# Depthwise convolution stage of a ConvNeXt block with a gate: matmul order kept as written, last 16 channels by halves of the images, norms ahead of their transposes

## The chip, the cores and the metric

The kernel runs on one core of one Trainium2 chip. The metric is device time in microseconds (us); the number for a kernel is the median of its runs. The kernel before takes 3158.46 us (three runs, 3158.37 to 3160.17). All data are float32.

## What is computed

The input x has 32 images of 384 channels and 28 x 28 pixels. Cut to what matters, the reference is:

```python
y = depthwise_conv7x7(x, dw_w) + dw_b            # padding 3, one 7x7 filter per channel
y = (y - mean_c(y)) * rsqrt(var_c(y) + 1e-6) * ln_g + ln_b   # over the 384 channels of a pixel
h = gelu(y @ w1 + b1)                            # 384 -> 1536
gx = sqrt(sum_pixels(h * h)); nx = gx / (mean_f(gx) + 1e-6)
h = grn_g * (h * nx) + grn_b + h
v = x + (h @ w2 + b2)                            # 1536 -> 384, residual
logits = concat(mean_hw(v) @ W1.T, group_max(v, W2_1) * W2_2, min_hw(v) @ W3.T) @ Wfc.T
out = sigmoid(logits[:, :, None, None] + v)
```

## The kernel before

**Engines.** PE (TensorE) does matmuls and transposes, ACT (ScalarE) and DVE (VectorE) empty PSUM and do element work, POOL (GpSimd) does element work in SBUF, SP only issues DMAs. A framework tracks which instruction needs which tile, inserts the semaphore waits, and also schedules: within an engine, instructions need not come in the order in which the Python code issues them, unless they are marked with `keep_in_program_order`. In the kernel before, none is marked.

**Stage 1: the convolution (L178 to L462).** The 7x7 filter of one channel becomes a banded matrix (`tmat`, loaded by `load_t`, L216, eight channels at a time, from a table of shifted taps `fs` in DRAM that is written at the start, L201 to L209). Pixels of four image rows, padded to 32 columns, lie on the 128 partitions; the seven such row blocks of 32 images are 224 columns. One channel is three matmuls into one PSUM area: the row block itself (L401, 224 columns), the block after (L402, 192 columns, 96 weight columns) and the block before (L405, 192). Each matmul shows as two records on PE.

The data come in with 32 channels of 4 images on the partitions: `load_x` (L235, on SP's queue, eight buffers `xi`), `pad_x` (L249: copied into one of two `xpad` buffers, by POOL for the first chunk at L253, then by ACT at L255), `turn_x` (L257: seven transposes at L264 into `pt`, three PSUM banks, in two halves, copied into `xt` by DVE at L272 or, in the first chunk, every second by ACT at L274). So stage 1 has 12 chunks of 32 channels, each chunk four steps `s` of eight channels, each step four pairs `c2` of two channels. While chunk k is convolved, the eight groups of chunk k + 1 are padded, turned and copied, one half-group after each pair. The result of a pair in `pc` (four banks) gets its bias on its way into `yc`, on DVE for odd pairs (L411) and on ACT for even ones (L419). Sixteen channels make a `yc`, which goes to DRAM: `yd` for the first 22 (L437), `yl` for the last 2 (L443), since the next stage wants all channels of one image. Image 0's part of the last channels is copied on the chip (L442) and its statistics taken (L441). Also in this stage, POOL forms sums of blocks of the two weight matrices (`form_w`, L324) and SP stores them to `u1d` and `u2d`.

**Between the stages (L867 to L873).** Image 0 is normalised: `stats` (L497), `std` (L509), then for each of seven row blocks j `norm` (L525, one instruction at L523 on ACT or L521 on DVE) and three transposes into `py` (L547, in `turn`); after j = 3 and j = 6 three copies take `py` to `acc` with scale and shift (L553). `forms_up` (L565, L587) makes ten sums and differences of `acc`'s blocks, on DVE for image 0 and on POOL for all others; they are the operands of the first matrix product, which is done in 15 block products instead of 18.

**Per image: `up` and `down`.** `up(b)` (L604) takes four tiles of the hidden layer in two pairs; for each pair it goes through the 15 entries of `UPSTEPS` (L92), two matmuls of 392 columns each (one a tile; two records a matmul, L627). An entry names the operand, the bank A, B or C that it adds to, and what is read from a bank afterwards (ACT copies at L634, DVE adds and subtracts at L636 to L644). `down(b)` (L696) is the second product, 15 entries of `STEPS`, four matmuls each (L717). All other work of the images is hung on these steps by two tables: `within(b)` (L794) for `up`, `beside(b)` (L832) for `down`: gelu (L596), squares (L602), scaling, the gate, and for image b + 2 the norms, transposes, evictions and `forms_up`. In the latter table, transposes of row blocks 0, 1 stand at step 0, of 2, 3 at step 1, of 4, 5 at step 2, of 6 at step 3; norms 0 and 1 are done in `up`, the others just ahead of their transposes. `yn`, the output of a norm, has three buffers.

Of the kernel before, what the change touches and what calls it, by code (L numbers as in the profile page):

```python
# [13 lines left out]
P = 128  # L14
# [50 lines left out]
)  # L65
EARLY = 7
# [26 lines left out]
    ("x", "+20", "A", 1, (("A", "copy", "2a"),)),  # L93
    ("p", "+20-21", "B", 1, (("B", "copy", "2b"),)),
    ("s", "-02", "C", 1, (("C", "copy", "0a"),)),
    ("v", "-12-20", "A", 0, (("A", "sub", "2b"),)),
    ("r", "-02+20-21", "B", 0, (("B", "sub", "2a"),)),
    ("2a", "-02+20+22", "C", 0, (("C", "add", "2a"),)),
    ("w", "-11+20", "A", 0, (("A", "copy", "E"),)),
    ("1a", "-01-20+21", "B", 0, (("B", "rsub", "E"),)),  # L100
    ("z", "-12", "C", 1, (("C", "add", "2b"),)),
# [20 lines left out]
def convnext_gate_kernel(  # L122
# [53 lines left out]


    with ExitStack() as one:  # L178
        tp = one.enter_context(tc.tile_pool(name="tp", bufs=1))
        xip = one.enter_context(tc.tile_pool(name="xip", bufs=8))  # L180
# [6 lines left out]
        ws = tp.tile([P, CB * FF], F32, name="ws")  # L187
        dww = tp.tile([P, CB, 49], F32, name="dww")
        nc.sync.dma_start(dww, dw_w.rearrange("(cb p) t -> p cb t", p=P))
        tab = tp.tile([P, CB, FL], F32, name="tab")  # L190
        dwb = tp.tile([P, C], F32, name="dwb")
        awt = tp.tile([P, 2, CB, R], F32, name="awt")
        w22b = tp.tile([P, R], F32, name="w22b")
        wfc = tp.tile([3 * R, C], F32, name="wfc")
        grp = tp.tile([P, CB, R], F32, name="grp")
        grp_a = tp.tile([P, CB, R], F32, name="grp_a")
# [5 lines left out]
        for cb in range(CB):  # L202
            nc.scalar.dma_start(fs[cb][P:, :], tab[:1, cb, :])
            nc.vector.tensor_copy(
                tab[:, cb, S0 : S0 + SN - 7].rearrange("p (y x) -> p y x", x=PW)[:, :, :7],
                dww[:, cb, :42].rearrange("p (y x) -> p y x", x=7),
            )
            nc.vector.tensor_copy(tab[:, cb, S0 + SN - 7 :], dww[:, cb, 42:])
            nc.scalar.dma_start(fs[cb][:P, :], tab[:, cb, :])  # L209
# [16 lines left out]
        NPAD = 2  # L226
# [4 lines left out]
        NG = B // NB  # L231
        GT = NX * NG
        xis = {}

        def load_x(i):  # L235

            k, g = divmod(i, NG)
            t = xis[i] = xip.tile([P, NT], F32, tag="xi", name=f"xi_{i}")
            base = x[g * NB, k * XC : k * XC + 1, :]
            nc.sync.dma_start(  # L240
                t,
                bass.AP(
                    tensor=base.tensor,
                    offset=base.offset,
                    ap=[[NT, XC], [C * NT, NB], [1, NT]],
                ),
            )
# [8 lines left out]

        def turn_x(i, h, xt, eng=nc.vector):  # L257
# [5 lines left out]
            for j in range(j0, j1):  # L263
                nc.tensor.transpose(  # L264
                    pt[:, j - j0, :],
                    xpad[i % NPAD][:, j * RW : (j + 1) * RW, :].rearrange("p r w -> p (r w)"),
                    ident,
                )
# [66 lines left out]

        AHEAD = NG
        for i in range(AHEAD):
            load_x(i)
        xt = new_xt(0)
        for i in range(NG):  # L340
# [4 lines left out]
            if i == NG - 2:  # L345

# [4 lines left out]
            for h in range(2):  # L351
                turn_x(i, h, xt, (nc.vector, nc.scalar)[h])

# [17 lines left out]
        GS = NG // SK  # L371
        for s in range(NK):
# [22 lines left out]
            t = tmat[s % NT2]  # L395
            for c2 in range(TC // 2):
                pc = psc.tile([P, 2, 256], F32, tag="pc", name=f"pc_{s}_{c2}")
                for ci in range(2):
                    c = 2 * c2 + ci
                    xc = xt[:, si * TC + c, :]  # L400
                    nc.tensor.matmul(pc[:, ci, :N], t[:, c, P : 2 * P], xc, start=True, stop=False)  # L401
                    nc.tensor.matmul(  # L402
                        pc[:REACH, ci, : N - B], t[:, c, 2 * P : T0 + MW], xc[:, B:], start=False, stop=False
                    )
                    nc.tensor.matmul(  # L405
                        pc[:, ci, B:N], t[:, c, :P], xc[:, : N - B], start=False, stop=True
                    )
                cc = s * TC + 2 * c2
                cy = cc % YC
                if c2 % 2:  # L410
                    nc.vector.tensor_tensor(  # L411
                        yc[:, :, :, cy : cy + 2].rearrange("p b j c -> p c j b"),
                        pc[:, :, :N].rearrange("p c (j b) -> p c j b", j=NJ),
                        dwb[:, cc : cc + 2].unsqueeze(2).unsqueeze(3).to_broadcast([P, 2, NJ, B]),
                        ALU.add,
                    )
                else:
                    for ci in range(2):
                        nc.scalar.activation(  # L419
                            yc[:, :, :, cy + ci].rearrange("p b j -> p j b"),  # L420
                            pc[:, ci, :N].rearrange("p (j b) -> p j b", j=NJ),
                            AF.Identity,
                            bias=dwb[:, cc + ci : cc + ci + 1],
                            scale=1.0,
                        )
                if xn is not None:
                    g, h = divmod(si * (TC // 2) + c2, 2)
                    i = (k + 1) * NG + g
                    if h == 0:
                        pad_x(i)  # L430
                        if i + AHEAD < GT:
                            load_x(i + AHEAD)
                    turn_x(i, h, xn)
            if s % 2:
                yv = yc.rearrange("p b j c -> p b (j c)")
                if kt < NY - NLAST:
                    nc.sync.dma_start(yd[:, kt], yv)  # L437
                else:
                    i = kt - (NY - NLAST)
                    for j in range(NJ):  # L440
                        nc.vector.bn_stats(bs0[:, j, 1 + i, :], yc[:, 0, j, :])  # L441
                    nc.vector.tensor_copy(yis[0][:, kt], yc[:, 0])  # L442
                    nc.sync.dma_start(yl[:, i], yv)  # L443
                if kt == NY - NLAST - 1:

                    yi = yis[0] = yip.tile([P, NY, NJ, YC], F32, tag="yi", name="yi_0")
                    nc.sync.dma_start(
                        yi[:, : NY - NLAST].rearrange("p k j c -> p k (j c)"), yd[:, :, 0, :]
                    )
                    bs0 = smp.tile([P, NJ, 1 + NLAST, 6], F32, tag="bs0", name="bs0", bufs=1)  # L450
                    for j in range(NJ):
                        nc.vector.bn_stats(bs0[:, j, 0, :], yi[:, : NY - NLAST, j, :])
            if si == SK - 1:
                xt = xn
            if s == SG:
# [13 lines left out]
    up1 = ctx.enter_context(tc.tile_pool(name="up1", bufs=6))  # L469
    up2 = ctx.enter_context(tc.tile_pool(name="up2", bufs=6))  # L470
# [3 lines left out]
    accp = ctx.enter_context(tc.tile_pool(name="accp", bufs=1))  # L474
# [8 lines left out]

    x_tiles, yts, sts, accs, pts, feats = {}, {}, {}, {}, {}, {}
    ssqs, gscs, gates, ys, ops, yns = {}, {}, {}, {}, {}, {}

# [3 lines left out]

    def load_y(b):
        yi = yis[b] = yip.tile([P, NY, NJ, YC], F32, tag="yi", name=f"yi_{b}")
        yk = yi.rearrange("p k j c -> p k (j c)")
        nc.sync.dma_start(yk[:, : NY - NLAST], yd[:, :, b, :])
        nc.sync.dma_start(yk[:, NY - NLAST :], yl[:, :, b, :])

    def stats(b):  # L497

        mv = sts[b] = smp.tile([P, NJ, 2], F32, tag="mv", name=f"mv_{b}")
        if b == 0:  # L500
            bs = bs0.rearrange("p j i v -> p j (i v)")
        else:
            bs = smp.tile([P, NJ, 6], F32, tag="bs", name=f"bs_{b}")
            for j in range(NJ):
                nc.vector.bn_stats(bs[:, j, :], yis[b][:, :, j, :])
        for j in range(NJ):
            nc.vector.bn_aggr(mv[:, j, :], bs[:, j, :])

    def std(b):  # L509
        mv = sts[b]  # L510
        sd = smp.tile([P, NJ], F32, tag="sd", name=f"sd_{b}")
        nc.scalar.activation(sd, mv[:, :, 1], AF.Sqrt, bias=eps_t, scale=1.0)
        rstd = smp.tile([P, NJ], F32, tag="rstd", name=f"rstd_{b}")
        nc.vector.reciprocal(rstd, sd)
        nmr = smp.tile([P, NJ], F32, tag="nmr", name=f"nmr_{b}")
        nc.vector.scalar_tensor_tensor(nmr, mv[:, :, 0], -1.0, rstd, ALU.mult, ALU.mult)
        sts[b] = rstd, nmr

    def affine(eng, out, in_, mul, add):
        if eng is nc.vector:  # L520
            eng.tensor_scalar(out, in_, mul, add, ALU.mult, ALU.add)  # L521
        else:
            eng.activation(out, in_, AF.Identity, bias=add, scale=mul)  # L523
# [10 lines left out]
    def turn(b, j, eng=nc.scalar, evac=(nc.scalar,) * CB):  # L534

        if (b, j) not in yns:
            norm(b, j, eng)
        yn = yns.pop((b, j))
        h = j // 4
        if j == 0:  # L540

            pool, tag = (xp, "x") if b == 1 else (accp, "acc")
# [379 lines left out]
```

## Time and profile before

| what | us |
|---|---|
| median of three runs | 3158.46 |
| the profiled execution | 3159.22 |
| its span | 3157.5 |
| PE busy in the span | 3108.3 (98%) |
| ACT, DVE, POOL busy | 1948.7, 1679.4, 1545.0 |
| first convolution matmul starts | 18.98 |
| last convolution matmul starts | 498.87 |
| first matmul of `up` starts | 513.35 |
| mean granted TensorE clock | 0.996 |

The span is the time from the first to the last instruction that the profile shows; what lies around it (1.7 us) belongs to the measured time too. A busy engine is one that has an instruction in work, and the end of a matmul is modelled; so a PE that is busy need not be at its peak, and time is better counted from start to start. `A <- B` in a wait means that A waited for B to finish.

### The profile page before, as it was taken

What the parts mean: (1) busy time and instruction counts of PE and PEld (TensorE: products, weight loads), DVE (VectorE), ACT (ScalarE), POOL (GpSimd) and SP (SyncE); (2) the same over time, 40 slices, a digit from 0 to 9 for tenths busy, and PEclk for the clock granted to TensorE, in tenths of its full rate; (3) what the DMA queues carried; (4) which work ended last, traced back from release to release, by engine and by line L of the source; (5) the groups of instructions that cost most, each with busy time, mean ns of one, the idle gap of its engine ahead of it and who ended that gap; (6) DMA issues with size and microseconds to landing.
All of it is one profiled execution on the core that took longest, in us unless ns stands there. A gap on an engine that the chain in (4) does not pass through costs nothing.

```text
span 3157.5 us, 34396 instructions
## 1 busy us (share of the span) xinstructions
PE 3108.3 (98%) x11459; PEld 2001.5 (63%) x11459; DVE 1679.4 (53%) x3446; ACT 1948.7 (62%) x3116; POOL 1545.0 (49%) x765
## 2 busy tenths in 40 slices
PE   8999998999999999999999999999999999999998
PEld 8999996555555555555555555555555555555555
DVE  3443435655555555555555555555555555555554
ACT  3333334766777666666666666666666666677762
POOL 1231301555555555555555555555555555555555
PEclk9999999999999999999999999999999999999999
DMA  9998975434444444444444444444444444444433
GB/s 363 364 359 337 348 279 202 133 114 143 143 145 138 135 143 145 145 140 148 140 148 140 148 140 148 140 147 141 133 138 133 145 145 145 142 144 139 134 103 131
DMA packets 294170, 540.79 MB, mean 171 GB/s; under 512 B 125135, under 2 KB 134890, under 8 KB 284906
## 3 DMA queue, kind: packets, MB, share of 16 engines
q1 hardware_dynamic: 281156, 500.72, 48.2%
q10 hardware_dynamic: 12838, 37.88, 3.2%
q8 instruction: 92, 1.51, 0.2%
q14 instruction: 84, 0.69, 0.1%
HBM read 447.53 MB, written 90.99 MB: 171 GB/s over the span
## 4 chain that ended last, share of the span: by engine, by line
PE 86%; ACT 11%; DVE 2%; issue 1%; DMA 1%; ACTq 0%; POOLq 0%; DVEq 0%; SPq 0%
PE ph_A L627 13%; PE ph_B L627 12%; PE ph_C L627 12%; PE pz_A L717 11%; PE pz_B L717 8%; PE pz_E L717 5%; PE pz_C L717 5%; ACT y L596 5%; PE pc L401 5%; PE pc L402 4%; PE pc L405 4%; PE pz_F L717 3%; ACT junk L602 3%; ACT acc L523 2%; ACT yn L523 2%; PE pt L264 2%
## 5 line engine op out<-in xcount | busy, mean ns | idle before, releaser
L596 ACT ACTIVATE y<-y,fv 128x784 f32<-128x784 f32 x384 | 347.7, 945 | 193.4 <-DVE y L642 170.7
L523 ACT ACTIVATE y<-y,fv,gsc 128x784 f32<-128x784 f32 x376 | 365.4, 1030 | 100.3 <-DVE gsc L663 100.3
L693 POOL TENSOR_TENSOR d_v<-d_u,y 128x1568 f32<-128x1568 f32 x32 | 112.6, 3520 | 588.7 <-PE pz_B L717 588.6
L602 ACT ACTIVATE junk<-y 128x784 f32<-128x784 f32 x384 | 328.2, 855 | 6.1
L627 PE MATMUL ph_A<-af,u 128*128 128x392 f32 x768 | 287.0, 496 | 6.0 <-DVE af L587 5.4
L627 PE MATMUL ph_B<-af,u 128*128 128x392 f32 x768 | 285.6, 494 | 0.0
L627 PE MATMUL ph_C<-af,u 128*128 128x392 f32 x768 | 284.4, 493 | 0.0
L717 PE MATMUL pz_A<-y,u 128*128 128x392 f32 x768 | 268.6, 492 | 0.0
L634 ACT ACTIVATE y<-ph_A 128x392 f32<-128x392 f32 x256 | 125.8, 493 | 217.0 <-PE ph_A L627 215.7
L752 POOL TENSOR_TENSOR zt<-gate,st 128x96 f32<-128x96 f32 x32 | 11.2, 351 | 468.4 <-PE ph_B L627 446.7
L636 DVE TENSOR_TENSOR y<-y,ph_C 128x392 f32<-128x392 f32 x384 | 216.1, 563 | 31.8 <-PE ph_C L627 1.0
L693 POOL TENSOR_TENSOR y<-d_v,y 128x1568 f32<-128x1568 f32 x64 | 223.7, 3516 | 2.4
L627 PEld LDWEIGHTS ph_A<-af,u 128*128 128x128 f32 x768 | 146.3, 191 | 113.9 <-DVE af L587 5.6
L401 PE MATMUL pc<-xt,tmat 128*128 128x224 f32 x768 | 210.1, 355 | 6.2 <-DVE yc L411 1.8
L627 PEld LDWEIGHTS ph_B<-af,u 128*128 128x128 f32 x768 | 146.4, 191 | 107.3 <-issue 1.3
L627 PEld LDWEIGHTS ph_C<-af,u 128*128 128x128 f32 x768 | 146.0, 190 | 107.7 <-DVE y L640 1.6
L717 PEld LDWEIGHTS pz_A<-y,u 128*128 128x128 f32 x768 | 145.8, 190 | 107.1 <-POOL y L693 0.5
L419 ACT ACTIVATE yc<-pc,dwb 128x224 f32<-128x224 f32 x192 | 102.5, 636 | 169.9 <-PE pc L405 166.8
L411 DVE TENSOR_TENSOR yc<-pc,dwb 128x448 f32<-128x448 f32 x96 | 89.8, 937 | 188.4 <-PE pc L405 154.7
L627 PE MATMUL ph_A<-acc,u 128*128 128x392 f32 x512 | 189.6, 492 | 0.0
L627 PE MATMUL ph_C<-acc,u 128*128 128x392 f32 x512 | 189.6, 492 | 0.0
L627 PE MATMUL ph_B<-acc,u 128*128 128x392 f32 x512 | 189.5, 492 | 0.0
(150 smaller groups left out, 6564.4 us busy)
## 6 DMA issues: line engine op xcount, KB each, us to landing
u<-u1d SPq DMA_DIRECT2D x384, 320.0 KB, 2.9
u<-u2d SPq DMA_DIRECT2D x480, 256.0 KB, 2.6
tmat<-fs SPq DMA_DIRECT2D x47, 1420.0 KB, 11.5
yd<-yc SPq DMA_DIRECT2D x22, 1792.0 KB, 6.6
yi<-yd SPq DMA_DIRECT2D x32, 1232.0 KB, 6.8
xi<-in_x SPq DMA_DIRECT2D x96, 392.0 KB, 10.9
x<-in_x SPq DMA_DIRECT2D x32, 1176.0 KB, 5.8
out<-x ACTq DMA_DIRECT2D x31, 1176.0 KB, 5.4
```

Of the source, the lines that this page charges most:

```text
L401: nc.tensor.matmul(pc[:, ci, :N], t[:, c, P : 2 * P], xc, start=True, stop=False)
L402: nc.tensor.matmul(pc[:REACH, ci, : N - B], t[:, c, 2 * P : T0 + MW], xc[:, B:], start=False, stop=False)
L405: nc.tensor.matmul(pc[:, ci, B:N], t[:, c, :P], xc[:, : N - B], start=False, stop=True)
L419: nc.scalar.activation(yc[:, :, :, cy + ci].rearrange("p b j -> p j b"), pc[:, ci, :N].rearrange("p (j b) -> p j b", j=NJ), AF.Identity, b ...
L523: eng.activation(out, in_, AF.Identity, bias=add, scale=mul)
L596: nc.scalar.activation(y, y, AF.Gelu, bias=b1_t[:, f : f + 1], scale=1.0)
L602: nc.scalar.activation(junk, ys[b][:, f, :], AF.Square, accum_out=ssqs[b][:, f : f + 1])
L627: nc.tensor.matmul(banks[t, bk][:, :NH], wts[t][:, i % UG, :], o[opnd], start=(first == 1), stop=True, skip_group_check=True,)
L634: nc.scalar.activation(d, p, AF.Identity)
L636: nc.vector.tensor_tensor(d, d, p, ALU.add)
L693: nc.gpsimd.tensor_tensor(d, o[in0], o[in1], op)
L717: nc.tensor.matmul(pz[:, :NH], wt[:, t, :], o[opnd][:, t, :], start=(first == 1 and t == 0), stop=(t == KT - 1), skip_group_check=True,)
```

## The change

1. **Order.** The matmuls of the convolution and the transposes of `turn_x` are marked to stay in program order on PE. The 16 half-groups of the next chunk are spread over the first 14 of a chunk's 16 pairs (`plan`). There are three `xpad` buffers instead of two, and a group is padded (and the load behind it issued) one group ahead of its transposes (`pad_next`).
2. **Start.** Only the first block's sequences are written to `fs` at once. Those of the other blocks and the zero rows follow at the seventh group of the first chunk, on ACT's queue. (The zero row has a place of its own, `zrow`.)
3. **Last 16 channels.** The steps 46 and 47 are done at the end, first for images 0 to 15, then for images 16 to 31. Between the pairs of the second half stand image 0's statistics (after the first pair), norms (second), transposes, evictions and forms (third and fourth). The first six loads of weights for `up` are issued between the halves. The second half of the last `yl` store goes on ACT's queue.
4. **`UPSTEPS`.** The order becomes p, s, x, r, 2a, v, z, w, 1a, 0b, then as before; `forms_up` makes its forms in the order p to x, z.
5. **Norms ahead.** `turn` is split into `norm`, `turn` (transposes alone) and `evac`. `within` does three norms of the image after the next, not two; `beside` has transposes 0, 1 at step 0; 2, 3 at step 1; 4, 5 at step 3; 6 at step 4; norms 3, 4 after the transposes of step 0, norms 5, 6 after those of step 1; evictions at steps 1 and 4, and `forms_up` at step 4.
6. **Memory.** To make room, buffers share places: `ws` (the weights of stage 1) later holds the rings of `u1` and one of six `u2` buffers, `room` holds seven of the `xi` buffers and later `acc` and the forms, small tables lie in a `yi` buffer (`scr`). The number of buffers of each kind in the image stage stays as it was.

```diff
 UPSTEPS = (
-    ("x", "+20", "A", 1, (("A", "copy", "2a"),)),
     ("p", "+20-21", "B", 1, (("B", "copy", "2b"),)),
     ("s", "-02", "C", 1, (("C", "copy", "0a"),)),
-    ("v", "-12-20", "A", 0, (("A", "sub", "2b"),)),
+    ("x", "+20", "A", 1, (("A", "copy", "2a"),)),
     ("r", "-02+20-21", "B", 0, (("B", "sub", "2a"),)),
     ("2a", "-02+20+22", "C", 0, (("C", "add", "2a"),)),
+    ("v", "-12-20", "A", 0, (("A", "sub", "2b"),)),
+    ("z", "-12", "C", 1, (("C", "add", "2b"),)),
     ("w", "-11+20", "A", 0, (("A", "copy", "E"),)),
     ("1a", "-01-20+21", "B", 0, (("B", "rsub", "E"),)),
-    ("z", "-12", "C", 1, (("C", "add", "2b"),)),
...
-        for cb in range(CB):
-            nc.scalar.dma_start(fs[cb][P:, :], tab[:1, cb, :])
+        def sequences(cb):
             nc.vector.tensor_copy(
...
-            nc.scalar.dma_start(fs[cb][:P, :], tab[:, cb, :])
+            return nc.scalar.dma_start(fs[cb][:P, :], tab[:, cb, :])
+
+        sequences(0)
...
-        NPAD = 2
+        NPAD = 3
...
+        def pad_next(i):
+            if i < GT:
+                pad_x(i)
+                if i + AHEAD < GT:
+                    load_x(i + AHEAD)
...
             if i == NG - 2:
+                for cb in range(CB):
+                    if cb:
+                        keep(sequences(cb))
+                    keep(nc.scalar.dma_start(fs[cb][P:, :], zrow))
...
+        pad_next(NG)
...
+        def conv(s, c2, yc, xt, b0, b1):
...
+                if nb == B:
...
+                else:
+                    po = pc[:, ci, : NJ * nb].rearrange("p (j b) -> p j b", b=nb)
+                    xc = xt[:, s % SK * TC + c, :].rearrange("p (j b) -> p j b", b=B)[:, :, b0:b1]
+                    after, before = xc[:, 1:], xc[:, : NJ - 1]
+                    lo, hi = po[:REACH, : NJ - 1], po[:, 1:]
+                keep(nc.tensor.matmul(po, t[:, c, P : 2 * P], xc, start=True, stop=False))
...
+        plan = [[] for _ in range(STEPS_K)]
+        for n in range(2 * NG):
+            plan[n * (STEPS_K - 2) // (2 * NG)].append(n)
+
+        def spread(k, q, xn):
+            for n in plan[q]:
+                g, h = divmod(n, 2)
+                i = k * NG + g
+                if h == 0:
+                    pad_next(i + 1)
+                turn_x(i, h, xn)
+
+        def first_image(n):
+            V, A = nc.vector, nc.scalar
+            if n == 0:
+                stats(0)
+                std(0)
+            elif n == 1:
+                rstd, nmr = sts[0]
+                for j in range(NJ):
+                    affine(
+                        (V, A)[j % 2], yn0[:, j, :].rearrange("p (k c) -> p k c", c=YC),
+                        yis[0][:, :, j, :], rstd[:, j : j + 1], nmr[:, j : j + 1],
+                    )
...
+            elif n in (2, 3):
+                h = n - 2
...
+                for cb in range(CB):
+                    untwist((A, V, A)[cb], room_acc, cb, j0, j1, py[cb])
+                if h:
+                    forms_up(0, V)
...
+                if s == NK - 1:
+                    for n in range(2 * PAIRS):
+                        conv(NK - 2 + n // PAIRS, n % PAIRS, yc, xt, 0, B0)
+                    store(yc, kt, 0, B0)
+                    for i in range(0, NS, UG):
+                        for t in range(2):
+                            first_u1[t, i] = load_u1(t, i)
+                    for n in range(2 * PAIRS):
+                        conv(NK - 2 + n // PAIRS, n % PAIRS, yc, xt, B0, B)
+                        first_image(n)
+                    if B0 < B:
+                        store(yc, kt, B0, B)
...
-            for j in range(2):
-                at((2, 26 + 2 * j), norm, b + 1, j)
+            for j in range(3):
+                at((2, 24 + 2 * j), norm, b + 1, j)
...
-            for j in range(NJ):
-                at((0, 0, 1, 1, 2, 2, 3)[j], turn, b + 2, j)
-            at(3, forms_up, b + 2)
+            for i, jj in enumerate(((0, 1), (2, 3), (), (4, 5), (6,))):
+                for j in jj:
+                    at(i, turn, b + 2, j)
+                for j in ((3, 4), (5, 6))[i] if i < 2 else ():
+                    at(i, norm, b + 2, j)
+                if i in (1, 4):
+                    at(i, evac, b + 2, i // 4)
+            at(4, forms_up, b + 2)
...
-    stats(0)
-    std(0)
-    for j in range(NJ):
-        turn(0, j, (A, V)[j % 2], (A, V, A))
-    forms_up(0, V)
-    if B > 1:
-        load_y(1)
```

## The prediction, made before the changed kernel was run

> **What bounds the kernel now.** I read the page's busy shares first (PE 3108.3 of 3157.5 us, 98%), so only PE's 49.2 idle us and whatever makes its matmuls slow can be won. Then the windows, to see where those lie (columns: length, then busy us of PE, PEld, DVE, ACT, POOL, the granted clock, DMA share, GB/s):
>
> ```profile
> 0.00:40.00 40.00, 29.05 (x180) 26.27 (x181) 15.14 (x26) 13.52 (x23) 8.44 (x22) 1.00 0.94 361
> ...
> 80.00:120.00 40.00, 39.67 (x252) 38.27 (x251) 17.36 (x28) 15.79 (x25) 8.68 (x9) 1.00 0.98 357
> ...
> 240.00:280.00 40.00, 38.01 (x229) 36.27 (x228) 14.50 (x21) 12.56 (x22) 2.76 (x2) 0.96 0.84 319
> ...
> 480.00:520.00 40.00, 29.42 (x143) 24.94 (x142) 21.25 (x59) 11.72 (x22) 0.00 (x0) 0.84 0.56 202
> ```
>
> PE is idle 10.95 us in the first slice and 10.6 in the slice of the transition; between 40 and 480 the slices sum to 9.3. A window from 560 to 2960 holds 7.7 more; about 10 lie in the last 37 us, which the change leaves alone. Then PE's waits, in 0:500, 500:560 and 560:3050 (total us, times, longest):
>
> ```profile
> PE pt L264 <- POOL xpad L253: 8.4, 5, 6.1
> PE pt L264 <- DVE xt L272: 3.9, 9, 0.4
> PE pc L401 <- DVE yc L411: 1.8, 1, 1.8
> PE pc L401 <- ACT xpad L255: 1.4, 3, 0.6
> PE pc L401 <- DVE xt L272: 1.4, 4, 0.3
> ```
> ```profile
> PE ph_A L627 <- DVE af L587: 5.4, 1, 5.4
> PE py L547 <- ACT yn L523: 4.6, 2, 4.3
> ```
> ```profile
> PE py L547 <- ACT yn L523: 8.0, 29, 0.3
> ```
>
> The last line is one wait of 0.28 us in 29 images. Last, PE's timeline at three such places (start, length, instruction, idle before it):
>
> ```profile
> 252.05 0.98 PE L264 MATMUL pt<-ident,xpad 128*128 128x128 f32 x7 [0.23 <-ACT xpad L255]
> 254.79 1.02 PE L401 MATMUL pc<-xt,tmat 128*128 128x224 f32 x2 [1.75 <-DVE yc L411]
> 255.60 0.85 PE L402 MATMUL pc<-xt,tmat 128*96 128x192 f32 x2
> ```
> ```profile
> 503.48 3.56 PE L547 MATMUL py<-ident,yn 128*128 128x128 f32 x18 [4.28 <-ACT yn L523]
> ...
> 513.35 1.68 PE L627 MATMUL ph_A<-af,u 128*128 128x392 f32 x2 [5.40 <-DVE af L587]
> ```
> ```profile
> 1430.77 0.49 PE L547 MATMUL py<-ident,yn 128*128 128x128 f32 x3
> 1431.54 0.55 PE L547 MATMUL py<-ident,yn 128*128 128x128 f32 x3 [0.28 <-ACT yn L523]
> ```
>
> Busy hides part of the loss, since a matmul's end is modelled. So I count by start-to-start: in undisturbed stretches a channel's six passes take 0.378 + 0.325 + 0.325 = 1.028 us, a transpose 0.109. From the first convolution (18.98) to the end of the last (499.04) are 480.1 us; 384 channels and 11 x 56 transposes need 394.8 + 67.1, three small transposes 0.3. So 17.9 us are lost: 1.0 soon after 18.98, some 15.3 in gaps at 8 places of about 0.6 between transposes and at the chunks' starts (0.5 to 1.9, with 1.8 of half clock after the 1.75 gap), 1.6 in scraps.
>
> [...] after 4.28 us idle, transposes came every 0.213 us, not 0.109; the 392-column passes after 513.35 every 0.65, not 0.327, up to 521.0. [...]
>
> **The change, part by part.**
>
> Start. Now the taps' copy waits 3.23 us (to 5.26) behind a store of the zero row; tmat_0 is issued at 11.27 and lands at 17.44. Writing only block 0's sequences first takes that wait away: -3.0. Bounds: -1 (the transfer is slowed by loads of x now beside it, DMA share 0.94) and -5 (SP's queue also blocked from 3.26 to 6.20). The two later blocks' issues stand ahead of ACT copies for group 6; their data are needed two chunks on. Padding one group ahead removes the two waits after the first convolution (0.6 and 0.4): -1.0 (0 to -1.6).
>
> Stage 1. A third xpad buffer, padding a step ahead, transposes at fixed places and the last of a chunk two pairs (4.1 us) before the first use: the 15.3 us of gaps should go, since the copy after a transpose takes 0.7. I leave 1.3 for scraps: -14 (-11 to -17). What is late next is DMA: its share is 0.94 to 0.99 up to 160 us, but tmat tiles land 12 to 20 us before use, and the shares times 40 us sum to 437 us of 480. Each pad's issue and the load of x behind it on SP move a step earlier, with its buffer.
>
> Transition. Last 16 channels by halves: [...] A channel-half takes 2 x (0.110 + 0.083 + 0.110) = 0.606; 32 of them 19.4 instead of 16.45: +2.9 (0 if loads overlap better, +5 if the strided operand is slower). This buys cover. Let T be the end of the first half: 499.04 - 16.45 + 9.7 = 492.3. From T: eviction 0.5, bn_stats 0.63, copy 0.2, aggregation 0.8, square root and two small ones 0.8 = norms from T+3.0, two engines at 0.5 to 0.7 each: four done by T+4.6. In PE's order the first 12 transposes come after three pairs of the second half (T+3.6): a wait near 0.9; then the rest. PE ends at T + 9.7 + 21 x 0.109 + 0.9 + 0.2 = T+13.1 = 505.4. Last untwist near T+8.5, ten forms on DVE 0.47 apart (508.54 to 513.2 before): p is there by T+9, all by T+13.2, and up takes p, s, x in this order. So up starts at 505.4 at full clock. Before, it is at full clock at 521.0 with 10 passes of 0.327 behind it, as if from 517.7. Gain 12.3 (bounds 7 and 14). New wait: the second half's yl store stands on ACT behind DVE's last eviction, with the untwists ahead of it, and behind it up's copies, not needed before T+16.9.
>
> Up's new order of steps. Four reuses of a bank move from three steps to two: 2 x 1.315 less one tile's 0.657 = 1.97 us for its eviction.
>
> ```profile
> L634 ACT ACTIVATE y<-ph_A 128x392 f32<-128x392 f32 x256 | 125.8, 493 | 217.0 <-PE ph_A L627 215.7
> ```
>
> That is 0.49 on ACT, and 1.36 at most from the matmul to the end of such a copy in images past 1, DVE 1.30. Nothing, except in image 0, where DVE also does image 1's statistics and norms: +1 (0 to +3).
>
> Middle. Norms of j = 3 to 6 are queued on ACT before the py evictions (3 in 1.94 us at 1428.96), and the split puts E's step between. 29 x 0.276 = -8.0 (-6 to -8.5, if one norm waits for a squaring of 0.86). Its evictions and POOL's forms come later; the forms would end near 1452 and up reads them at 1464, so 12 us cover. Without cover the forms' delay, some 2 us, would count per image.
>
> Sum: -3.0 - 1.0 - 14 - 12.3 + 1 - 8.0 = -37.3. Against the profiled execution: 3157.5 - 37.3 = 3120.2 of span, and 1.7 around it (3159.22 - 3157.5) give 3121.9. The profiled run stands 0.76 above the median of 3158.46; from that, 3121.
>
> **Rivals.**
> (A) DMA binds stage 1. For: 0.98 in 40 to 160. Against: PE is idle only 1.1 us there. If the gain is 5 instead of 14: 3130.
> (B) The transition's chain isn't covered: DVE's and ACT's queues mix evictions of the second half with norms, and forms end late. Gain 5 instead of 12.3: 3128. For: 1 us of slack. Against: both engines are under half busy there.
> (C) Slower: the shortened reuse of banks in up. If ACT or DVE is late at those spots, PE stalls in each of 64 blocks of two tiles: 1 us a block gives 3121 + 64 = 3185. It decides from 43.6 / 64 = 0.68 us a block (37.3 and the 6.3 that 0.2% is). For: gelu at 0.945 and norms stand ahead of copies on ACT. Against: at most 1.36 measured against 1.97.
> (D) The order does little: the gaps come from late copies, not PE's order, and stay as other waits. Gain 0 of the 14: 3135.
>
> **How the numbers follow.** Forecast 0.65 (3112 to 3130), A 0.11, B 0.10, C 0.06, D 0.06, and 0.02 for several at once near no change. Low end: all parts at their good bounds, -5 - 1.6 - 17 - 14 - 8.5 = 3112. High end: 3136, which takes in A, B and D and leaves C out. Faster by over 0.2% (6.3 us, about what a measurement tells from no change): 0.91; within 0.2%: 0.03, slower 0.06.
>
> **What would show it.** First convolution near 16 instead of 18.98, no PE wait over 0.3 us between 40 and 480, chunk starts 39.1 us apart; from 490 on no idle stretch over 1.5 us and the clock at 1.0 in 480 to 520; first ph near 486 (505.4 less 18 gained earlier); no py <- yn wait in the middle. Wrong if ph waits for ACT or DVE in the middle (C), pc waits for tmat or pt for xpad (A, D), or ph for af near 490 (B).

## The result and the profile after

The changed kernel takes 3122.96 us (median of four runs, 3122.18 to 3123.67), the kernel before 3158.41 (median of four, measured beside it): 35.5 us less, a ratio of 0.9887 with a 95% interval of 0.9869 to 0.9904. The prediction said 3121. The sum was nearly right, but two of its terms were far off: the start brought nothing where 4 us were expected, and the middle brought 14.6 where 8.0 were expected. The profiled execution took 3123.22 with a span of 3121.5.

The windows of the changed kernel (length, busy us of PE, PEld, DVE, ACT, POOL, granted clock, DMA share, GB/s), at the slices shown of before:

```profile
0.00:40.00 40.00, 30.45 (x169) 28.30 (x170) 14.07 (x26) 13.27 (x23) 8.56 (x23) 0.91 0.94 349
...
80.00:120.00 40.00, 40.00 (x256) 38.84 (x255) 16.71 (x27) 15.29 (x26) 9.05 (x10) 1.00 0.98 350
...
240.00:280.00 40.00, 38.48 (x245) 37.16 (x244) 15.39 (x23) 14.02 (x24) 4.25 (x3) 1.00 0.91 351
...
480.00:520.00 40.00, 37.84 (x213) 27.53 (x212) 29.39 (x83) 18.06 (x37) 0.00 (x0) 1.00 0.70 224
```

PE is busy all of 80:120 at the same DMA share of 0.98. The transition's slice went from 29.42 to 37.84 busy, at full clock. The first slice has more busy time than before, but at a clock of 0.91 instead of 1.00: that is no gain. (Neither figure counts the time up to the first rise of the clock, at 11.94 and before at 9.16, in which PE runs at half pace, a transpose every 0.213 us, not 0.109; see the last section.) PE's waits in 0:480 and 480:560; for 560:3050 none is listed:

```profile
PE pt L386 <- POOL xpad L372: 6.0, 1, 6.0
PE pc L529 <- ACT xt L397: 3.4, 1, 3.4
PE pc L529 <- issue: 1.5, 1, 1.5
```
```profile
PE ph_B L774 <- DMA yi<-yl: 1.5, 1, 1.5
PE py L608 <- ACT xt L234: 0.4, 1, 0.4
```

All the waits of stage 1's steady part are gone but one of 1.5 us, for which the profile shows no releaser. It stands in every kernel below that keeps the order, before the first matmul of the channel with index 184 (counted from 0), and there the kernel before waits as well (1.75 us, at 254.79). Why is not known.

```profile
248.01 0.49 PE L386 MATMUL pt<-ident,xpad 128*128 128x128 f32 x3
250.01 0.62 PE L529 MATMUL pc<-xt,tmat 128*128 128x224 f32 x2 [1.52 <-issue]
```

Two waits are new or grown: 3.4 us before the first convolution (0.6 before), and 1.5 us before the first matmul of `up`, which now stands right behind stage 1.

To see where the time came from, I cut PE's timeline of each kernel (of its one profiled execution) by the starts of four matmuls, so that nothing depends on the modelled ends: chunk 2's first convolution, the first of the last 16 channels, the first of `down`, PE's last. In us:

| kernel | start to chunk 2 | chunk 2 to the last 16 channels | those, transition, first two `up` | rest |
|---|---|---|---|---|
| before | 60.87 | 421.71 | 117.25 | 2550.04 |
| after | 61.57 | 409.24 | 107.61 | 2535.47 |
| difference | +0.70 | -12.47 | -9.64 | -14.57 |
| predicted | -4.0 | -14 | -11.3 | -8.0 |

The four differences sum to -35.98, as the span's does (3157.5 to 3121.5). The same table for the experiments:

| kernel | start | steady stage 1 | transition | rest | median less that of before, measured beside it |
|---|---|---|---|---|---|
| after | 61.57 | 409.24 | 107.61 | 2535.47 | -35.5 |
| e1, late writes on SP | 58.42 | 409.25 | 107.63 | 2535.61 | -38.1 |
| e2, evictions on ACT | 60.68 | 409.24 | 106.75 | 2535.47 | -35.8 |
| e3, norms at old steps | 60.95 | 409.24 | 107.64 | 2549.84 | -20.5 |
| e4, order free | 61.96 | 415.12 | 110.83 | 2535.50 | -25.9 |
| e5, two xpad buffers | 59.17 | 409.25 | 107.68 | 2535.63 | -37.8 |
| e6, no halves | 61.10 | 409.24 | 109.95 | 2535.49 | -34.7 |
| e7, old steps of up | 61.45 | 409.24 | 106.94 | 2535.49 | -37.7 |
| e8, three edits | 57.23 | 409.24 | 106.75 | 2535.64 | -39.9 |
| e9, norms alone, on before | 60.60 | 421.67 | 117.79 | 2535.54 | -15.5 |
| e10, no halves, old steps | 61.39 | 409.24 | 114.83 | 2535.61 | -28.0 |
| e11, no padding ahead | 61.08 | 409.24 | 108.84 | 2535.65 | -33.3 |
| e12, order and spread only | 59.52 | 409.24 | 108.90 | 2535.49 | -34.8 |

Medians are of four runs, of before of four or seven. Single runs of a kernel lie up to 4.3 us apart and before's median moved by up to 1.7 from one measurement to the next, so differences of some 2 us are read from the segments. Where kernels share the code of a segment, these agree within 0.2 us, but for the start: the changed start, as it is in the first row, in e2, e3, e6, e7 and e10, gives 60.68 to 61.57.

### The profile page after: what moved, and what is told of

It reads as the page before. It is cut to its first block, busy times and chain, and to the rows that moved or that the text cites. A ratio compares the mean times of both kernels' runs of the same rounds, so it can differ in the third digit from the quotient of the medians.

```text
span 3121.5 us, 34685 instructions
## 1 busy us (share of the span) xinstructions
PE 3097.7 (99%) x11555; PEld 2005.6 (64%) x11555; DVE 1683.8 (54%) x3452; ACT 1953.1 (63%) x3123; POOL 1542.5 (49%) x766
## 3 DMA queue, kind: packets, MB, share of 16 engines
q8 instruction: 93, 1.52, 0.2%
## 4 chain that ended last, share of the span: by engine, by line
PE 98%; DMA 1%; ACT 1%; DVE 0%; issue 0%; ACTq 0%; SPq 0%; POOLq 0%; DVEq 0%
PE ph_B L774 13%; PE ph_C L774 13%; PE ph_A L774 13%; PE pz_A L859 11%; PE pz_B L859 11%; PE pz_E L859 5%; PE pz_C L859 5%; PE pc L529 5%; PE pc L533 4%; PE pc L531 4%; PE pz_F L859 3%; PE pz_D L859 3%; PE pz_G L859 3%; PE py L732 2%; PE pt L386 2%; DMA dwb<-in_cvec 0%
## 5 line engine op out<-in xcount | busy, mean ns | idle before, releaser
L774 PE MATMUL ph_B<-room,ws 128*128 128x392 f32 x1240 | 458.9, 492 | 1.5 <-DMA yi<-yl 1.5
L774 PE MATMUL ph_C<-room,ws 128*128 128x392 f32 x1240 | 459.0, 492 | 0.0
L774 PE MATMUL ph_A<-room,ws 128*128 128x392 f32 x1240 | 458.9, 492 | 0.0
L774 PEld LDWEIGHTS ph_B<-room,ws 128*128 128x128 f32 x1240 | 235.4, 190 | 173.6 <-issue 1.8
L774 PEld LDWEIGHTS ph_A<-room,ws 128*128 128x128 f32 x1240 | 235.5, 190 | 172.8 <-ACT y L781 0.6
L774 PEld LDWEIGHTS ph_C<-room,ws 128*128 128x128 f32 x1240 | 235.3, 190 | 172.2 <-DVE y L787 0.4
L269 POOL TENSOR_TENSOR room<-room 128x392 f32<-128x392 f32 x300 | 294.3, 1015 | 2.3
L529 PE MATMUL pc<-xt,tmat 128*128 128x224 f32 (+1 forms) x800 | 213.8, 349 | 4.9 <-ACT xt L397 3.4
L533 PE MATMUL pc<-xt,tmat 128*128 128x192 f32 (+1 forms) x800 | 192.9, 323 | 0.0
L531 PE MATMUL pc<-xt,tmat 128*96 128x192 f32 (+1 forms) x800 | 191.1, 321 | 0.0
## 6 DMA issues: line engine op xcount, KB each, us to landing
room<-in_x SPq DMA_DIRECT2D x84, 392.0 KB, 11.3
```

The costliest lines, as they stand in the source:

```text
L269: eng.tensor_tensor(d, o[in0], o[in1], op)
L529: keep(nc.tensor.matmul(po, t[:, c, P : 2 * P], xc, start=True, stop=False))
L531: nc.tensor.matmul(lo, t[:, c, 2 * P : T0 + MW], after, start=False, stop=False)
L533: keep(nc.tensor.matmul(hi, t[:, c, :P], before, start=False, stop=True))
L774: nc.tensor.matmul(banks[t, bk][:, :NH], wts[t][:, i % UG, :], o[opnd], start=(first == 1), stop=True, skip_group_check=True,)
```

## The experiments

**Start (e1).** In the changed kernel ACT's timeline shows the late writes and the copy behind them; PE's shows what waits (start, length, instruction, idle before it). ACTq is ACT issuing a DMA.

```profile
14.77 0.36 ACTq L321 DMA_DIRECT2D fs<-ws  x1
...
18.16 0.24 ACTq L479 DMA_DIRECT2D fs<-scr  x1
18.44 0.87 ACT L397 ACTIVATE xt<-pt 128x384 f32<-128x384 f32 x2 [3.77 <-DMA fs<-scr]
```
```profile
7.79 8.20 PE L386 MATMUL pt<-ident,xpad 128*128 128x128 f32 x48
19.37 1.12 PE L529 MATMUL pc<-xt,tmat 128*128 128x224 f32 x2 [3.38 <-ACT xt L397]
20.28 0.85 PE L531 MATMUL pc<-xt,tmat 128*96 128x192 f32 x2
```

The fifth issue stands in ACT's queue until 18.16, and the last two copies into `xt`, whose transposes were done at 16.0, stand behind it. PE then waits 3.38 us, and its clock is half until 25 (passes of 192 columns every 0.32 us, 0.163 otherwise). The edit takes the five issues from ACT and puts them on SP's queue, two steps later:

```diff
-            if i == NG - 2:
-                for cb in range(CB):
-                    if cb:
-                        keep(sequences(cb))
-                    keep(nc.scalar.dma_start(fs[cb][P:, :], zrow))
...
+            if s == 1:
+                for cb in range(CB):
+                    if cb:
+                        sequences(cb, nc.sync)
+                    nc.sync.dma_start(fs[cb][P:, :], zrow)
             if s in later:
```

> The changed kernel, with the five late writes of the sequences and zero rows taken from ACT's queue in the first chunk and put on SP's queue two steps later. Theory (start): the last of these five issues waited on ACT for a transfer, kept the last copy into xt back to 18.44, and so cost a wait of 3.4 us before the first convolution (19.37) and some 3 us of half clock until 25. Then the first convolution starts at 16.5 to 17.3, the clock holds, and the kernel takes 3117 to 3119 (4 to 6 less than 3122.96). Rival: the first convolution waits for its weights or x anyway (first tmat half landed at 15.3, second at 17.0): start near 19 and 3122 to 3123.

Measured: 3119.35 us, 38.1 below before. PE's timeline:

```profile
17.83 0.65 PE L524 MATMUL pc<-xt,tmat 128*128 128x224 f32 x2 [0.58 <-ACT xt L397]
...
21.37 0.98 PE L386 MATMUL pt<-ident,xpad 128*128 128x128 f32 x7 [1.21 <-ACT xpad L374]
```

The mechanism holds: no half clock (passes of 192 columns come every 0.16 us from 18.32 on) and a start 1.5 us earlier; chunk 2 begins 3.15 us earlier than in the changed kernel (2.3 to 3.15 us earlier than in the six kernels with the changed start). The size was below the 4 to 6 expected: the first convolution came at 17.83, not by 17.3, in an execution whose clock rose late (transposes at half pace until 14.34, in the changed kernel until 11.94), and a wait of 1.21 us came in for group 8 (the first of chunk 2), whose load lands late (the pad waits for it until 20.46).

**Bank handover (e2).** The wait before `up`'s first matmul is put down to a DMA. DVE's timeline of the changed kernel says otherwise:

```profile
489.81 3.91 DVE L269 TENSOR_TENSOR room<-room 128x392 f32<-128x392 f32 x8
493.63 0.54 DVE L537 TENSOR_TENSOR yc<-pc,dwb 128x224 f32<-128x224 f32 x1
494.00 1.03 DVE L269 TENSOR_TENSOR room<-room 128x392 f32<-128x392 f32 x2
494.94 0.53 DVE L537 TENSOR_TENSOR yc<-pc,dwb 128x224 f32<-128x224 f32 x1
```

The last eviction of stage 1 ends at 495.47, behind the ten forms, and the matmul starts at 495.73. Among its waits in the program is that eviction.

```diff
-            if c2 % 2:
+            if c2 % 2 and not (s == NK - 1 and b0):
                 nc.vector.tensor_tensor(
```

> The changed kernel, with all evictions of the second half of the last 16 channels on ACT. Theory: the 1.5 us wait before up's first matmul (put down to a DMA by the profile) is DVE's last eviction, queued behind image 0's ten forms, whose bank that matmul takes over. Then the wait shrinks to 0 to 0.7 us and the kernel takes 3121.4 to 3122.3. Rival (the profile's name): the DMA of image 1's y or the weights of up: the wait stays 1.5 us, time 3123.

Measured: 3121.57, 35.8 below before; the transition's segment 0.86 shorter. The wait now bears another name and is shorter, as the theory has it, though not by all of it:

```profile
PE ph_B L774 <- ACT yc L545: 0.8, 1, 0.8
```

From start to start, the pause between the last convolution's passes and `up` went from 1.7 us to 1.0. So some 0.7 of it was DVE's queue; the rest is the last eviction itself, now on ACT, which follows the last convolution in any case. The median alone (35.8 against 35.5) would not tell the two apart.

**Norms (e3 and e9).** e3 puts the old tables back in the changed kernel; e9 puts the new ones into the kernel before (the mirror of this edit, with the eviction split off `turn`).

```diff
-            for j in range(3):
-                at((2, 24 + 2 * j), norm, b + 1, j)
+            for j in range(2):
+                at((2, 26 + 2 * j), norm, b + 1, j)
...
-            for i, jj in enumerate(((0, 1), (2, 3), (), (4, 5), (6,))):
...
-            at(4, forms_up, b + 2)
+            for j in range(NJ):
+                i = (0, 0, 1, 1, 2, 2, 3)[j]
+                if j > 1:
+                    at(i, norm, b + 2, j)
+                at(i, turn, b + 2, j)
+                if j in (3, NJ - 1):
+                    at(i, evac, b + 2, j // 4)
+            at(3, forms_up, b + 2)
```

> The changed kernel, with norms, transposes, evictions and forms of the later images at their old steps (part 5 undone). Theory (start-to-start count): each of 29 images loses 0.44 to 0.5 us, so 3122.96 + 14.4 = 3137.3. Rival (the wait's own length of 0.28, as the prediction had it): 3122.96 + 8.0 = 3131.

> The kernel before with the new places of norms, transposes, evictions and forms of the later images alone. Theory: the same 0.495 us for each of 29 images as in the changed kernel, so 14.4 below before. Rival (the wait's own length): 8.0 below.

Measured: e3 3136.93, 20.5 below before; rest of the timeline 2549.84, that is 14.37 more than the changed kernel. e9 3143.60, 15.5 below before (ratio 0.9952, 0.9937 to 0.9967); rest 14.50 less than before. Both ways the theory's 14.4, not 8.0. Yet e3's waits show the old line again:

```profile
PE py L732 <- ACT yn L234: 8.0, 29, 0.3
```

So the same wait is 0.28 us in this view and 0.50 on the clock: 14.37 / 29. In the kernel before, the three transposes at 1430.77 need 3 x 0.109 = 0.33 and the next starts at 1431.54: 0.44 lost. The listed idle begins at the modelled end (1430.77 + 0.49), which comes later than PE could have gone on. The other 0.06 lies behind the gap: the three transposes at 1431.54 take 0.38, not 0.33, up to the next matmul,

```profile
1431.92 2.80 PE L717 MATMUL pz_E<-d_s,u 128*128 128x392 f32 x8
```

and so in all 29 images, in which the first transpose after the gap takes 0.165 until the next one starts and all others take 0.109. In e9 no wait for `yn` is listed in 560:3050, and the transposes run on:

```profile
1432.47 0.49 PE L547 MATMUL py<-ident,yn 128*128 128x128 f32 x3
1432.80 1.48 PE L721 MATMUL pz_E<-y,u 128*128 128x392 f32 x4
```

**Order in stage 1 (e4, e5, e11, e12).** e4 takes the marks off the convolution's matmuls and the transposes.

```diff
-                keep(nc.tensor.matmul(po, t[:, c, P : 2 * P], xc, start=True, stop=False))
+                nc.tensor.matmul(po, t[:, c, P : 2 * P], xc, start=True, stop=False)
...
```

> The changed kernel, with the marks that keep PE's order in stage 1 taken off; three xpad buffers, padding ahead and the spread of the half-groups stay. Theory: the order is what removes the gaps of stage 1, so most of its 14 us come back: 3130 to 3138. Rival: buffers and padding ahead do it, whatever the order: within 2 us of 3123.

Measured: 3131.52, 25.9 below before. That is inside the range expected, but not for the reason given: the steady part takes only 5.88 us more than with the marks, under half of the 12.47 that it had gained. Another 3.22 are lost in the transition, where PE now waits 3.6 us instead of 1.5 before `up` and has half clock for 3.4. PE's timeline with free order, then the changed kernel's:

```profile
210.15 0.49 PE L529 MATMUL pc<-xt,tmat 128*128 128x192 f32 x2
210.48 1.25 PE L385 MATMUL pt<-ident,xpad 128*128 128x128 f32 x10
212.17 0.30 PE L385 MATMUL pt<-ident,xpad 128*128 128x128 f32 x1 [0.44 <-DVE xt L393]
```
```profile
245.51 0.60 PE L386 MATMUL pt<-ident,xpad 128*128 128x128 f32 x4
245.95 0.54 PE L529 MATMUL pc<-xt,tmat 128*128 128x224 f32 x2
246.33 0.49 PE L531 MATMUL pc<-xt,tmat 128*96 128x192 f32 x2
```

Left free, the scheduler bunches half-groups: ten transposes in a row fill the three banks of `pt`, and the eleventh waits for DVE's copy (seven such waits between 0 and 480). Kept, a half-group is followed by a pair (2.06 us here), in which the copy (0.69) has time. e5, e11 and e12 take the helpers away, one by one and both:

```diff
-        NPAD = 3
+        NPAD = 2
```
```diff
-        pad_next(NG)
...
-                    pad_next(i + 1)
+                    pad_next(i)
```

> The changed kernel with two xpad buffers instead of three. Theory: kept order and padding a group ahead are enough; a pad then has to wait for the transposes of one pair before and has some 4 us for its 0.86: within 1.5 us of the changed kernel (35.5 below before). Rival: the third buffer is what ends the waits for xpad: waits of pt on xpad come back in most chunks, 4 us or more slower than the changed kernel.

> The changed kernel with each group padded just ahead of its own transposes instead of one group ahead; order and three buffers stay. Theory: with the order kept, padding ahead is what makes room; without it PE waits for ACT's pad of 0.86 and what stands before it in each of 88 groups: over 40 us slower than the changed kernel. Rival: ACT runs far enough ahead by itself: within 3 us.

> The changed kernel with two xpad buffers and each group padded just ahead of its own transposes: of the edits to stage 1's steady part, only the kept order and the spread of the half-groups stay. Theory: order and spread do it alone, so no waits of pt on xpad in the middle of stage 1, and the time is within 2 us of the kernel with three buffers and no padding ahead (33.3 below before). Rival: either a third buffer or padding ahead is needed to let ACT run ahead: waits of pt on xpad in most groups, 5 us or more slower.

Measured: 3121.32, 3124.91 and 3123.79; 37.8, 33.3 and 34.8 below before. The steady part is 409.24 or 409.25 us in all three: with the order kept, neither the third buffer nor padding ahead is worth anything there. My theory of e11, 40 us slower, fell outright. e5 came out 2.3 us below the changed kernel by medians, where at most 1.5 either way was expected; by segments all of that is the start. What brings the 6.6 us of the steady part that stay with free order (421.71 to 415.12) was not taken apart: the spread without the marks, and the marks without the spread, were not run. The 1.2 and 1.3 us that e11 and e12 lose in the transition go with a `py` wait of 2.0 us instead of 0.4, which I did not follow up. In e5 and e12 the start is 2 us shorter although the late writes are still on ACT: the transposes end later, PE waits 2.13 and 1.43 for the copy instead of 3.38, and the clock isn't lost (passes of 192 columns every 0.16 us from the first on). First e5, then e12:

```profile
18.71 0.65 PE L529 MATMUL pc<-xt,tmat 128*128 128x224 f32 x2 [2.13 <-ACT xt L397]
19.20 0.49 PE L531 MATMUL pc<-xt,tmat 128*96 128x192 f32 x2
```
```profile
18.20 0.65 PE L528 MATMUL pc<-xt,tmat 128*128 128x224 f32 x2 [1.43 <-ACT xt L397]
```

**Halves and order of steps (e6, e7, e10).** e6 convolves the last 16 channels for all images at once, e7 puts the old `UPSTEPS` and the old order of forms back, e10 does both.

```diff
-        B0 = min(B, 16)
+        B0 = B
```
```diff
-UPFORMS = "pqrstuvwxz"
+UPFORMS = "pqwrstuvxz"
...
+    ("x", "+20", "A", 1, (("A", "copy", "2a"),)),
     ("p", "+20-21", "B", 1, (("B", "copy", "2b"),)),
     ("s", "-02", "C", 1, (("C", "copy", "0a"),)),
-    ("x", "+20", "A", 1, (("A", "copy", "2a"),)),
...
```

> The changed kernel with the last 16 channels convolved for all images at once, image 0's statistics, norms, transposes and forms after them. Theory: the halves cost PE 3.6 us (32 x 0.626 instead of 16.45), but without them the chain of some 15 to 19 us stands uncovered, with the clock lost: 7 to 10 us slower than the changed kernel. Rival: most of the chain's gain comes from norms without the ring of three buffers and from the order of forms, not from cover: within 4 us of it.

> The changed kernel with the old order of up's steps and of image 0's forms. Theory: evictions have room in both orders, so no difference from the third image on; image 0's first step then needs x, the ninth form, which DVE has by then: within 1.5 us of the changed kernel. Rival: the new order's shorter reuse of banks costs time in each pair of tiles: the old order is 2 us or more faster.

> The changed kernel with the last 16 channels for all images at once and the old order of up's steps and of the forms. Theory: halves and the order of forms stand in for each other. With neither, the first step waits for the ninth form, some 4 us more than with the whole images alone, and half clock on top: 4 to 6 us slower than that kernel (34.7 below before), so 29 to 31 below before. Rival: the order of forms brings nothing here either (as with the halves): 34 to 35 below before.

Measured: e6 3124.46, 34.7 below before; e7 3121.47, 37.7 below; e10 3130.23, 28.0 below. The rival of e6 was right: with the new order in place, the halves are worth only 2.34 us by segment, 0.8 by median. e10's theory held by segment, 4.88 us more than e6; by median it is 6.7 and just outside the range. PE's waits of e6, then e10:

```profile
PE py L608 <- DVE xt L232: 3.9, 1, 3.9
PE ph_B L774 <- issue: 1.4, 1, 1.4
```
```profile
PE ph_A L774 <- DVE room L269: 5.2, 1, 5.2
PE py L608 <- DVE xt L232: 3.8, 1, 3.8
```

With the old order, `up` waits 5.2 us for the ninth form; with the new one it starts on the first. With halves as well, PE is busy while the forms are made, and the order has nothing left to win: old order with halves (106.94) is even 0.67 below the changed kernel. So with the old order the halves are worth 7.9 us (114.83 less 106.94), with the new one 2.3: either edit does most of what both do. e7's median lies 2.2 us below the changed kernel's, which is what its rival forecast, but the segments do not bear the rival out: after the first two `up` the two kernels differ by 0.02 us in 2535, so the shorter reuse of banks costs nothing in the images.

**The best version (e8).** e1's and e2's edits, and every second pad of the first chunk on ACT:

```diff
-            if i < NG:
+            if i < NG and i % 2 == 0:
                 nc.gpsimd.tensor_copy(dst, src)
```

> The changed kernel with three edits: the five late writes on SP's queue, the second half's evictions on ACT, and in the first chunk every second pad on ACT instead of POOL. Theory: the first two bring what they brought alone (2.9 and 0.9 us); with them the transposes of the first chunk are paced by POOL's pads, so that sharing these lets the first convolution start near 16 instead of 17.8: 3122.96 - 2.9 - 0.9 - 1.5 = 3117.7 (40 to 41 below before). Rival: the loads of x set the pace and the first convolution stays at 17.5 to 18: 3119.

Measured: 3118.34 (3117.88 to 3118.76), 39.9 below before; ratio 0.9872 (0.9857 to 0.9887). The first convolution starts at 16.79, 1.04 us earlier than in e1, and chunk 2 at 57.23. That sharing the pads brought this is not shown: PE's clock rose at 11.95 here and at 14.34 in e1, and until then a transpose takes 0.213 us, not 0.109. The changed kernel, with all pads on POOL and the rise at 11.94, even starts the last of these transposes earlier (15.71 against 15.93). A wait of 0.98 for group 8's load remains:

```profile
16.79 0.65 PE L524 MATMUL pc<-xt,tmat 128*128 128x224 f32 x2 [0.58 <-ACT xt L397]
...
20.09 0.98 PE L386 MATMUL pt<-ident,xpad 128*128 128x128 f32 x7 [0.98 <-ACT xpad L374]
```

It is the fastest kernel of this study, 4.4 us further below before than the changed one. The old order of steps (e7), worth 0.67 beside the halves, was not tried in it.

## Why the prediction was right in sum, and where it was wrong

Start, -3.0 and -1.0: wrong, +0.70, and that is within what the same start varies by. What failed is the sentence that the later blocks' issues stand ahead of ACT copies for group 6 and their data are needed two chunks on. The weights did land earlier (the first half of `tmat` at 15.26, not 17.44), but I asked when the late writes' data are needed, not how long the issue itself stays in ACT's queue. It stayed until 18.16, and the copies with it: their transposes were done at 16.0, and they start at 18.44, right behind the issue. The half clock came on top (18.77 to 25.60). The gain was there: e1 has 2.45 of it and e8 3.64 (60.87 less 58.42 and 57.23). The -1.0 for padding one group ahead is not shown either: where the start comes early, the transposes of group 8 wait 1.21 (e1) and 0.98 us (e8) for its load, against 0.63 before.

Stage 1, -14: measured -12.47. The mechanism was right, the cause one edit smaller: the order and the spread suffice (e12), and 5.88 of it goes when the marks alone go (e4). The chunks start 39.05 or 39.06 us apart in eight of ten cases, as forecast. What is missing is in the main the wait of 1.5 at 250.01, which was counted among the gaps that would go and stayed: its chunk takes 40.81. DMA was no bound (A): its share is 0.98 in 80:120 with PE busy 40.00 of 40. D is refuted as well: it gave the 14 nothing.

Transition with image 0, -12.3 and +1: measured -9.64, that is -10.2 up to `up`'s first matmul (with before counted, as the prediction does, as if from 517.7) and +0.6 from there to the first of `down`. Mis-sized was the price of the halves:

```profile
471.41 0.40 PE L529 MATMUL pc<-xt,tmat 128*128 128x112 f32 x2
471.65 0.33 PE L531 MATMUL pc<-xt,tmat 128*96 128x96 f32 x2
471.82 0.39 PE L533 MATMUL pc<-xt,tmat 128*128 128x96 f32 x2
...
477.69 0.40 PE L529 MATMUL pc<-xt,tmat 128*128 128x112 f32 x2
```

112-column passes came every 0.12 us, not 0.110, and ten channel-halves took 6.28 (471.41 to 477.69), so 32 x 0.628 - 16.45 = +3.6 instead of +2.9. Not seen at all was the 1.7 us at `up`'s first matmul: the bank that it takes must first be emptied (1.0 in e2), and forms stood in front of that eviction (0.7). The chain was otherwise as worked out: the wait at `py` 0.82 by starts (0.9 predicted). That cover brings the gain is right, but it isn't the only way to it: e10 keeps 2.4 of the 9.64 with neither halves nor new order; from there the halves alone bring 7.9 (e7), the order alone 4.9 (e6), both together 7.2. B's mechanism, forms and evictions mixed in DVE's queue, cost 0.7, not 7.

Middle, -8.0: mechanism right, size wrong, -14.57. The failed term is "29 x 0.276". I had counted stage 1 by starts because busy hides part of the loss, and here took the listed idle nevertheless. By the two lines shown of 1430.77 and 1431.54 it would have been 0.44 x 29 = 12.8, and with the slow transpose behind the gap 0.50 x 29 = 14.4.

C, the rival on the slower side, is refuted by e7. Three terms missed on the one side (start 4.7 us, stage 1 1.5, transition 1.7) and one on the other (middle 6.6), and they nearly cancelled: that 3121 lies 2 us from 3122.96 is in good part luck.

Three details of the prediction need a correction or a source. 505.4 less 18 is 487.4, not 486; the first matmul of `up` came at 495.73, late by the misses before it (4.7, 1.5 and 2.1). The 0.110 and 0.083 a pass were an estimate from the weight loads near 3079.6 of before, of 128 columns, which start 0.110 apart (the two passes of one column there start 0.03 apart): 0.083 is 0.110 x 96 / 128. The 96-column passes here came out close to it, 0.111 behind 128 weight columns and 0.084 behind 96. And after the wait of 4.28 us before, the first six transposes still came at full pace (503.48 to 504.08); the next twelve came every 0.213.

## What to carry to other kernels

Price a wait on PE from start to start, not by the idle that the waits list, wherever the end of an instruction is modelled. Before a DMA issue is put on a computing engine's queue, ask what that issue waits for and what stands behind it there. When several edits aim at one wait, take them away singly and together: here halves and order of forms stood in for each other, and a buffer and padding ahead did nothing in the steady part once the order was kept.

## What the runs showed of the hardware

PE starts slow: the first transposes come every 0.213 us, not 0.109, until the clock rises, at 9.16 us of the span in the kernel before and at 11.94 in the changed one (11.95 in e8, 14.34 in e1). The record of the granted clock begins only there, and the windows show 1.00 for what lies before it (0:9 of before).

In the changed kernel PE waited 3.38 us before the first convolution (up to 19.37), and the record has half clock from 18.77 to 25.60. After waits there of 0.58 us (before, e1, e8), 1.43 (e12) and 2.13 (e5) the passes of 192 columns came every 0.16 us, at full pace. But length alone does not decide: in the kernel before, a wait of 1.75 us at 254.79 was followed by half clock from 254.92 to 258.33; the one of 1.52 at 250.01 in the changed kernel was not (1.00 in 248:255). Nor does the price follow it: 6.83 us at half clock behind the wait of 3.38, and 3.41 (504.09 to 507.51) behind the 4.28 of before. In e5 the first convolution came 0.66 us earlier than in the changed kernel, and chunk 2, with the clock kept, 2.4.

A pass of 112 columns with a strided moving operand took 0.125 and 0.112 us in turn; with 96 columns it took 0.111 behind 128 weight columns and 0.084 behind 96. A transpose that followed a wait of PE for its data took 0.165 us until the next, where the others took 0.109, in 29 of 29 images of before.
